# Moving a range check from the second convolution into the output stage of an attention and quantized-convolution kernel

## The chip, the cores and the metric

The kernel runs on one core of a Trainium2 chip, in one launch. The metric is the device time of a run in microseconds (us). Names of engines: PE (TensorE matmul), DVE (VectorE), ACT (ScalarE), POOL (GpSimd), SP (SyncE, which here issues transfers). L1074 means line 1074 of the kernel before; in the kernel after, the lines of the output stage have numbers smaller by three (L1139 is L1136), and those behind it are larger by three (L1326 is L1329).

## The reference

The input x is 16 images of 128 channels and 32 x 32 pixels in float32. Two layers follow each other.

```python
# layer 0: four-head attention over the 1024 pixels of an image
q, k, v = split(einsum('bchw,oc->bohw', x, w_qkv) + b_qkv)
attn = softmax(q @ k * c ** -0.5)
x = einsum(attn @ v, w_out) + b_out + x
# layer 1: two quantized convolutions with batch norm, and a residual
out = conv3x3(act_quant(x), weight_quant(w1))
out = conv3x3(act_quant(batchnorm(out)), weight_quant(w2))
return batchnorm(out) + x
```

The batch norm takes mean and variance over all images, so nothing of the last stage can start before the last image has left the second convolution.

## The kernel before

The softmax is computed without subtracting a maximum, which is exact as long as the sums of exponentials stay in a sane range. The kernel therefore has two paths. `fast_path` computes everything. A check of the reciprocal sums (`check_sums`, L352) writes a flag, and behind `fast_path` every engine loads the flag (L1326) and branches on it (L1327) over `general_attention` and `quantized_convs`, a slower general path that writes the output again. With this input the flag is 0 and all engines take the branch over it.

`fast_path` has four stages. First the attention of 16 images with the first convolution interleaved; it ends at about 1921 us, with the last image's first convolution until 1926. Attention results go to memory (`x_dram`), ten of the first convolution's results too (`y_dram`). Then `bn_params(0)`, and the second convolution from 1929 to 1989.5 us, image by image. Then `bn_params(1)`, and last the output stage: ACT applies scale and bias (L1136, L1138), DVE adds the residual (L1139), SP writes the result (L1140). The residual comes back from memory as `x1` (named `res`), one transfer of 7.5 MB that is under way until about 1957 us.

In the second convolution most images are nine shifted matmuls per half of the image (`conv`, L277, 18 matmuls). Images 3, 5, 7, 9, 11 and 13 are "filtered": four combinations of rows, three matmuls each (`filtered_conv`, L1078). What an image needs is prepared some images ahead by `quantize2(b)` (L1050): ACT writes `steps` (L1058), DVE clips them (L1059), and DVE (L1063, images below 6) or ACT (L1065) writes the padded image, `pad` or, for a filtered one, `padf`. For a filtered image four row combinations follow (L1074), two on DVE and two on POOL. After its matmuls ACT copies an image out of PSUM (L293) or DVE and ACT combine the filtered parts (L1094 to L1098), and DVE takes its statistics (L298).

The order on each engine's queue is not the order of the text alone: a planner places instructions by its estimate of when they can run. `tc.issue_after(x)` holds an instruction behind the instruction x in that order. All queues run in order, so an instruction that waits holds all that stand behind it.

The check consists of eleven small DVE instructions (L349 to L369), one POOL instruction that takes the maximum over the partitions (L371), and one DVE copy of the result into the integer flag (L372). Before POOL's instruction and again before POOL's next row combination the program has an instruction pair that changes POOL's configuration, which the trace shows as MODIFY_POOL_CONFIG under L371 and L1074. The check is called in the loop of the second convolution, behind the statistics of image 1:

```python
if b == 1:
    with tc.issue_after(done.ins):
        check_sums()
```

Of the kernel before, what the change touches and what calls it, by code (L numbers as in the profile page):

```python
# [12 lines left out]
ALU = mybir.AluOpType  # L13
# [180 lines left out]
def fast_path(  # L194
# [18 lines left out]
    B, C, N = x.shape  # L213
# [57 lines left out]
    def gather(n):  # L271
        nc.vector.bn_aggr(late[n][:, 1:3], early[n].rearrange("p g s -> p (g s)"))
        nc.vector.tensor_scalar(
            late[n][:, 2:3], late[n][:, 2:3], float((B - 1) * N), None, ALU.mult
        )

    def conv(pool, tag, b, n, r, rows=RPH, group=None, after=None):  # L277

        ps = pool.tile([P, rows, W], F32, tag=tag, name=f"psc{n}_{b}_{r}")
        for tap in range(NTAP):  # L280
            dy, dx = divmod(tap, 3)
            last = nc.tensor.matmul(  # L282
                ps,
                lhsT=wq[n][:, tap, :],
                rhs=pads[b % NPAD][:, r + dy : r + dy + rows, dx : dx + W],
                start=(tap == 0),
                stop=(tap == NTAP - 1),
            )
        ps = ps.rearrange("p h w -> p (h w)")
        if group is not None:  # L290
            with tc.issue_after(after) if after else nullcontext():
                nc.vector.bn_stats(place(n, b, group), ps)
        nc.scalar.copy(ys[b][:, r * W : (r + rows) * W], ps)  # L293
        return last

    def statistics(b, n):
        for hf in range(NHF):
            last = nc.vector.bn_stats(place(n, b, hf), ys[b][:, ts(hf, HALF)])  # L298
        return last
# [47 lines left out]
    def sums_range(b):  # L347
        flat = sums[:, b * NH : (b + 1) * NH, :].rearrange("p g k -> p (g k)")
        nc.vector.tensor_reduce(ext[:, 0, b : b + 1], flat, AX.X, ALU.min)  # L349
        nc.vector.tensor_reduce(ext[:, 1, b : b + 1], flat, AX.X, ALU.max)  # L350

    def check_sums():  # L352

        sums_range(B - 1)
        ok = keep.tile([P, 2], F32, name="ok")
        low, high = keep.tile([P, 1], F32, name="low"), keep.tile([P, 1], F32, name="high")
        nc.vector.tensor_reduce(low, ext[:, 0, :], AX.X, ALU.min)
        nc.vector.tensor_reduce(high, ext[:, 1, :], AX.X, ALU.max)
        nc.vector.tensor_scalar(ok[:, 0:1], low, 1.0 / SUM_LIMIT, None, ALU.is_ge)
        nc.vector.tensor_scalar(ok[:, 1:2], high, SUM_LIMIT, None, ALU.is_le)  # L360
        bad = keep.tile([P, 1], F32, name="bad")
        nc.vector.tensor_tensor(bad, ok[:, 0:1], ok[:, 1:2], ALU.mult)
        even = keep.tile([P, B], F32, name="even")
        nc.vector.scalar_tensor_tensor(
            even, ext[:, 0, :], SUM_RATIO, ext[:, 1, :], ALU.mult, ALU.is_ge
        )
        nc.vector.tensor_reduce(ok[:, 0:1], even, AX.X, ALU.min)
        nc.vector.tensor_tensor(bad, bad, ok[:, 0:1], ALU.mult)
        nc.vector.tensor_scalar(bad, bad, -1.0, 1.0, ALU.mult, ALU.add)  # L369
        worst = keep.tile([P, 1], F32, name="worst")  # L370
        nc.gpsimd.partition_all_reduce(worst, bad, P, bass_isa.ReduceOp.max)  # L371
        nc.vector.tensor_copy(flag, worst[0:1, :])  # L372

    with ExitStack() as ph:
        pool = lambda name, bufs, **kw: ph.enter_context(tc.tile_pool(name=name, bufs=bufs, **kw))
# [550 lines left out]
        for g in range(LAST):  # L926
            b, h = heads[g]
# [79 lines left out]
    with ExitStack() as ph:  # L1007
# [38 lines left out]
        x1 = resp.tile([P, B, N], F32, name="res")  # L1046
# [3 lines left out]
        def quantize2(b, r0=0, r1=H):  # L1050

            pad = filtered_pads[FILTERED.index(b) % 2] if b in FILTERED else pads[b % NPAD]
            t = steps.tile([P, (r1 - r0) * W], BF16, tag="steps", name="steps")
            y = ys[b][:, r0 * W : r1 * W]
            if (b, r0) == (0, 0):
                nc.vector.tensor_scalar(t, y, scale1, bias1, ALU.mult, ALU.add)
            else:
                nc.scalar.activation(t, y, AF.Identity, bias=bias1, scale=scale1)  # L1058
            nc.vector.tensor_scalar(t, t, STEP, STEP + A_LEVELS, ALU.max, ALU.min)  # L1059
            into = pad[:, r0 + 1 : r1 + 1, 1 : W + 1]  # L1060
            t = t.rearrange("p (h w) -> p h w", w=W)
            if b < 6:
                done = nc.vector.tensor_scalar(into, t, STEP, None, ALU.subtract)  # L1063
            else:
                nc.scalar.activation(into, t, AF.Identity, bias=down)  # L1065
            if b not in FILTERED:
                return done if b < 6 else None
            rows[b] = rowp.tile([P, 4, D, W + 2], BF16, tag="rows", name=f"rows2_{b}")
            pick = lambda r: pad[:, r : r + 2 * D - 1 : 2, :]
            four = ((0, 2, ALU.subtract), (1, 2, ALU.add), (2, 1, ALU.subtract), (1, 3, ALU.subtract))  # L1070
            for k in (1, 2, 0, 3):
                x, y, op = four[k]
                engine = nc.vector if k in (1, 2) else nc.gpsimd
                engine.tensor_tensor(rows[b][:, k], pick(x), pick(y), op)  # L1074
# [3 lines left out]
        def filtered_conv(b):  # L1078
            m = [None] * 4
            for k in (1, 2, 0, 3):  # L1080
                m[k] = ps_c.tile([P, D, W], F32, tag="c", name=f"psf_{b}_{k}")
                for dx in range(3):
                    nc.tensor.matmul(  # L1083
                        m[k],
                        lhsT=weights[k][:, dx, :],
                        rhs=rows[b][:, k, :, dx : dx + W],
                        start=(dx == 0),
                        stop=(dx == 2),
                    )
            y = ys[b].rearrange("p (i r w) -> p r i w", r=2, w=W)  # L1090
            new = lambda what: sump.tile([P, D, W], F32, tag=what, name=f"{what}_{b}")

            half, total = new("half"), new("total")
            nc.scalar.mul(half, m[1], 0.5)  # L1094
            nc.vector.scalar_tensor_tensor(total, m[2], 0.5, half, ALU.mult, ALU.add)
            nc.vector.tensor_tensor(y[:, 0], m[0], total, ALU.add)
            nc.vector.scalar_tensor_tensor(half, m[2], -0.5, half, ALU.mult, ALU.add)
            nc.vector.tensor_tensor(y[:, 1], half, m[3], ALU.subtract)  # L1098
# [8 lines left out]
        for b in range(B):  # L1107
            if b in FILTERED:
                filtered_conv(b)
            else:  # L1110
                ends = starts.get(b, (0, RPH, H))
                for i, (r0, r1) in enumerate(zip(ends, ends[1:])):
                    conv(ps_c, "c", b, 1, r0, r1 - r0, group=i if b == B - 1 else None)
            if b + 2 < B and b + 2 not in FILTERED:
                quantize2(b + 2)
            if b + 4 in FILTERED:
                quantize2(b + 4)
            if b < B - 1:
                done = statistics(b, 1)
            if b == 1:  # L1120
                with tc.issue_after(done.ins):
                    check_sums()
            if b == B - 2:
                gather(1)
        scale2, bias2 = bn_params(1)
# [3 lines left out]
        for b in range(B):  # L1129
            ends = parts.get(b, (0, N))  # L1130
            for lo, hi in zip(ends, ends[1:]):
                y = ys[b][:, lo:hi]
                if b == 0 and hi <= N // 2:
                    nc.vector.tensor_scalar(y, y, scale2, bias2, ALU.mult, ALU.add)
                elif b < 2:
                    nc.scalar.activation(y, y, AF.Identity, bias=bias2, scale=scale2)  # L1136
                elif lo == 0:
                    nc.scalar.activation(ys[b], ys[b], AF.Identity, bias=bias2, scale=scale2)  # L1138
                nc.vector.tensor_tensor(y, y, x1[:, b, lo:hi], ALU.add)  # L1139
                nc.sync.dma_start(out=out[b][:, lo:hi], in_=y)  # L1140
    outer.close()


# [105 lines left out]
def attention_then_quantized_convs(  # L1249
# [49 lines left out]
    def conv_weights(n, wp, behind):  # L1299
# [19 lines left out]

    flag = const.tile([1, 1], mybir.dt.int32, name="flag")  # L1320
    fast_path(
        nc, tc, x, wqk, wvo, bo, bnp, x1d, y1d, out, bo_sb, bnp_sb, quad, wq, sc, flag, conv_weights,
        constants,
# [82 lines left out]
```

## Time and profile before

| what | value |
|---|---|
| median of 3 runs | 2019.51 us (2019.31 to 2022.78) |
| the profiled execution, its own time | 2020.26 us |
| span of the profiled execution | 2018.2 us |
| mean granted TensorE clock | 0.994 |
| busy over the span | PE 98%, DVE 87%, ACT 59%, POOL 1% |
| second convolution, first to last matmul | 1929.2 to 1989.5 us |
| output stage, first output add to last landing | 1992.6 to 2016.8 us |

The span is what the profile sees of one execution; the time of the same execution is 2.06 us longer. Every moment below is counted from the start of the span. "Landing" of a transfer is when its completion is seen; a row of the timeline names at its end, in brackets, how long the engine was idle ahead of it and which instruction ended that. PE's busy share is high over the whole, but the last 90 us have to be read stage by stage.

### The profile page before, as it was taken

To read this page: it belongs to the slowest core of one execution; us is meant where nothing else is said; L and a number is where in the kernel's file an instruction comes from. 1 tells how busy PE (TensorE), PEld (TensorE's weight loads), DVE (VectorE), ACT (ScalarE), POOL (GpSimd) and SP (SyncE) were. 2 spreads that over 40 slices of the span, in tenths; PEclk is the share of its full clock that TensorE was granted. 3 is DMA by queue.
4 is the path that set the end of the run, shared out by engine and by line. 5 is a ranking of instruction groups with operands and counts; after the bars stand their busy time and mean duration, and the time that the engine had idled before them with its cause. 6 is when DMAs were issued, how large, how long until landed. Compare 5 with 4: busy or idle time off the path is not lost.

```text
span 2018.2 us, 25220 instructions
## 1 busy us (share of the span) xinstructions
PE 1980.9 (98%) x9676; PEld 890.9 (44%) x9677; DVE 1746.7 (87%) x2753; ACT 1193.5 (59%) x1992; POOL 19.6 (1%) x29
## 2 busy tenths in 40 slices
PE   9999999999999999999999999999999999999994
PEld 3466444444434444444444444444444444444442
DVE  4889898898988889889888988888898988989888
ACT  3565665665566566566556556656655665665575
POOL 0000000000000000000000000000000000000020
PEclk9999999999999999999999999999999999999997
DMA  1000000000000000000000000000000000000074
GB/s 42 24 1 22 1 22 1 22 1 0 22 0 22 1 7 26 1 21 11 22 11 1 32 1 21 11 21 11 1 32 1 22 11 22 11 1 22 1 281 168
DMA packets 13937, 47.96 MB, mean 24 GB/s; under 512 B 1521, under 2 KB 1905, under 8 KB 13809
## 3 DMA queue, kind: packets, MB, share of 16 engines
q1 hardware_dynamic: 10608, 36.25, 4.8%
q10 hardware_dynamic: 3200, 10.03, 1.6%
q8 instruction: 77, 1.26, 0.3%
q14 instruction: 52, 0.42, 0.1%
HBM read 24.25 MB, written 22.02 MB: 23 GB/s over the span
## 4 chain that ended last, share of the span: by engine, by line
PE 97%; DVE 1%; ACT 0%; issue 0%; DMA 0%; POOL 0%; DVEq 0%; ACTq 0%
PE pss L404 44%; PE psa L404 38%; PE psu L404 6%; PE psv L404 5%; PE psc L282 2%; PE psw L404 2%; PE psf L1083 1%; DVE back L1139 1%; DVE y L1139 0%; DMA x<-in_x_dram 0%; POOL rows L1074 0%; ACT y L1136 0%; PE ps_a L404 0%; PE psr L404 0%; ACT u L510 0%
## 5 line engine op out<-in xcount | busy, mean ns | idle before, releaser
L404 PE MATMUL pss<-u,x 128*64 128x512 f32 (+1 forms) x4128 | 1033.2, 590 | 1.6 <-ACT u L510 1.6
L404 PE MATMUL psa<-e,vo 128*64 128x512 f32 (+1 forms) x3624 | 922.4, 588 | 0.0
L552 ACT ACTIVATE e<-pss 128x512 f32<-128x512 f32 x1008 | 598.0, 597 | 373.4 <-PE pss L404 371.3
L404 PEld LDWEIGHTS pss<-u,x 128*64 128x64 f32 x4128 | 402.1, 137 | 492.3 <-issue 432.7
L404 PEld LDWEIGHTS psa<-e,vo 128*64 128x64 f32 x3624 | 359.9, 137 | 417.8 <-issue 389.5
L556 DVE TENSOR_TENSOR e<-e 128x1024 f32<-128x1024 f32 x252 | 308.1, 1223 | 29.0 <-ACT e L552 21.7
L555 DVE TENSOR_TENSOR e<-e 128x512 f32<-128x512 f32 x252 | 171.5, 680 | 92.2 <-ACT e L552 91.8
L559 DVE TENSOR_TENSOR e<-e 128x512 f32<-128x512 f32 x252 | 173.4, 688 | 18.2 <-DVE e L556 0.5
L596 ACT COPY ev<-psa 128x512 f32<-128x512 f32 x252 | 135.4, 589 | 88.9 <-PE psa L404 87.8
L404 PE MATMUL psu<-x,at_sb 128*64 128x512 f32 x512 | 185.9, 600 | 0.5 <-DMA x<-in_x_dram 0.5
L404 PE MATMUL psv<-bt_sb,x 128*64 128x512 f32 x512 | 184.9, 592 | 1.0 <-ACT bt_sb L481 1.0
L531 ACT COPY vo<-psv 128x512 f32<-128x512 f32 x128 | 75.7, 591 | 142.2 <-PE psv L404 142.2
L565 DVE TENSOR_TENSOR es<-es,e 128x1024 f32<-128x1024 f32 x126 | 154.0, 1222 | 2.2
L510 ACT ACTIVATE u<-psu,au_sb 128x512 f32<-128x512 f32 x127 | 87.6, 690 | 21.2 <-PE psu L404 19.6
L609 DVE TENSOR_TENSOR y<-ev,y 128x512 f32<-128x512 f32 x63 | 43.3, 687 | 52.4 <-ACT y L607 52.4
L404 PEld LDWEIGHTS psv<-bt_sb,x 128*64 128x64 f32 x512 | 58.8, 137 | 63.0 <-issue 55.3
L404 PEld LDWEIGHTS psu<-x,at_sb 128*64 128x64 f32 x512 | 58.9, 138 | 61.5 <-issue 56.8
L665 DVE STREAM_TRANSPOSE rb<-sums 128x1024 f32<-128x1024 f32 (+1 forms) x66 | 80.0, 1211 | 2.1
L835 ACT COPY m<-psw 128x512 f32<-128x512 f32 x45 | 26.4, 587 | 92.4 <-PE psw L404 91.4
L626 DVE TRANSPOSE_TENSOR_REDUCE part<-es 128x32 f32<-128x1024 f32 (+1 forms) x65 | 79.6, 1225 | 0.6
L563 DVE TENSOR_TENSOR es<-e,e 128x1024 f32<-128x1024 f32 x63 | 76.8, 1219 | 0.0
L676 DVE TENSOR_TENSOR av<-av,rb 128x1024 f32<-128x1024 f32 x47 | 57.6, 1225 | 1.6
(165 smaller groups left out, 1234.9 us busy)
## 6 DMA issues: line engine op xcount, KB each, us to landing
x_dram<-acc SPq DMA_DIRECT2D x16, 512.0 KB, 4.2
x<-in_x_dram ACTq DMA_DIRECT2D x15, 512.0 KB, 4.6
res<-x_dram SPq DMA_DIRECT2D x1, 7680.0 KB, 34.4
y_dram<-y SPq DMA_DIRECT2D x10, 512.0 KB, 2.6
back<-y_dram SPq DMA_DIRECT2D x1, 5120.0 KB, 16.6
out_dram<-back SPq DMA_DIRECT2D x10, 512.0 KB, 4.3
out_dram<-y SPq DMA_DIRECT2D x9, 256.0 KB, 2.4
raw<-in_cw_dram ACTq DMA_DIRECT2D x2, 576.0 KB, 4.2
```

Source lines behind the costliest of these rows:

```text
L404: done = nc.tensor.matmul(out_, lhsT=lhsT, rhs=rhs, start=start, stop=stop)
L510: copied = nc.scalar.activation(dst, ps, AF.Identity, bias=au_sb[:, h : h + 1])
L531: nc.scalar.copy(v[:, c : c + 3 : 2], ps.rearrange("p (h a o) -> p a h o", a=2, o=PH))
L552: exps[:] = [nc.scalar.activation(e[:, 2 * c + 1 - m], ps, AF.Exp).ins]
L555: nc.vector.tensor_tensor(e[:, T3], e[:, B12], e[:, B22], ALU.add)
L556: nc.vector.tensor_tensor(e[:, T1 : T2 + 1 : T2 - T1], e[:, B12 : B11 + 1], e[:, B11 : T3 + 1 : T3 - B11], ALU.subtract)
L559: nc.vector.tensor_tensor(e[:, T4], e[:, T2], e[:, B21], ALU.add)
L563: nc.vector.tensor_tensor(sides[g], es[g, 0][:, T4 : T3 + 1], mine, ALU.add)
L565: added = nc.vector.tensor_tensor(sides[g], sides[g], mine, ALU.add)
L596: nc.scalar.copy(to, ps)
L626: nc.vector.tensor_reduce(part, total.rearrange("p (k c) -> p k c", c=Q), AX.X, ALU.add, apply_transpose=True,)
L665: nc.vector.transpose(rb, rinv.unsqueeze(2).to_broadcast([P, n, Q]))
```

## The change

`check_sums` no longer copies the flag; it returns `worst`. Its call moves from the second convolution into the output stage, behind the add of image 4 (B // 4). The copy into the flag follows behind the add of image 13 (B - 3, the fourteenth image). On POOL the all-reduce now stands behind all row combinations, and the configuration is changed once instead of twice. On SP the load of the flag now stands behind all output writes. The new order on DVE in the output stage is: the adds of images 0 to 4; L349, L350, L357; add of image 5; L358, L359, L364, L360; add of 6; L362; add of 7; L367; add of 8; L368; add of 9; L369; adds of 10 to 13; the copy of the flag; adds of 14 and 15. The planner also moves some instructions of the second convolution: DVE's L1059 of image 6 now stands behind L1098 and the second row sum of image 7 and behind the statistics of image 3, where before it stood between L1095 and L1096 of image 3; on ACT L1065 of image 6 stands behind the copies of image 4.

```diff
@@ check_sums
         nc.gpsimd.partition_all_reduce(worst, bad, P, bass_isa.ReduceOp.max)
-        nc.vector.tensor_copy(flag, worst[0:1, :])
+        return worst
@@ the loop of the second convolution
             if b < B - 1:
                 done = statistics(b, 1)
-            if b == 1:
-                with tc.issue_after(done.ins):
-                    check_sums()
             if b == B - 2:
                 gather(1)
@@ the loop of the output stage
-                nc.vector.tensor_tensor(y, y, x1[:, b, lo:hi], ALU.add)
+                added = nc.vector.tensor_tensor(y, y, x1[:, b, lo:hi], ALU.add)
                 nc.sync.dma_start(out=out[b][:, lo:hi], in_=y)
+            if b == B // 4:
+                with tc.issue_after(added.ins):
+                    worst = check_sums()
+            if b == B - 3:
+                with tc.issue_after(added.ins):
+                    nc.vector.tensor_copy(flag, worst[0:1, :])
```

## The prediction

> **What bounds the kernel now.** I read the page first, then the timeline around the check, engine by engine, then the chain, the DMA view and the order of instructions on each queue before and after. The page says the whole is TensorE (PE 98%). The change touches only the last 90 us, so I read PE there. Columns: start us, length us, engine, line, operation, and in brackets the idle time before it and who ended it.
>
> ```profile
> 1941.13 1.48 PE L1083 MATMUL psf<-rows,middle 128*128 128x512 bf16 x6
> 1942.45 1.49 PE L1083 MATMUL psf<-rows,wq 128*128 128x512 bf16 x6
> 1945.52 4.14 PE L282 MATMUL psc<-pad,wq 128*128 128x512 bf16 x18 [1.58 <-DVE pad L1063]
> 1949.50 1.48 PE L1083 MATMUL psf<-rows,middle 128*128 128x512 bf16 x6
> 1952.99 0.82 PE L1083 MATMUL psf<-rows,wq 128*128 128x512 bf16 x3 [2.02 <-POOL rows L1074]
> 1954.27 0.82 PE L1083 MATMUL psf<-rows,wq 128*128 128x512 bf16 x3 [0.45 <-POOL rows L1074]
> 1954.92 4.13 PE L282 MATMUL psc<-pad,wq 128*128 128x512 bf16 x18
> ```
>
> PE waits three times, for image 4's pad and twice for image 5's rows; from 1954.27 to 1989.5 it has no gap. Without waits an 18-matmul image takes 3.97 us in the chain and a filtered one 2.64, so image 4 could have started at 1941.13 + 2.64 = 1943.77 (1.75 lost), image 5's second half at 1945.52 + 3.97 + 1.32 = 1950.81 (2.18 lost), its last three matmuls 0.66 after 1952.99 (0.62 lost): **4.55 us lost**. The DVE and POOL rows say why.
>
> ```profile
> 1940.43 0.43 DVE L1063 TENSOR_SCALAR padf<-steps 128x1024 bf16<-128x1024 bf16 x1
> 1943.15 0.14 DVE L372 CAST flag<-worst 1x1 int32<-1x1 f32 x1 [2.29 <-POOL worst L371]
> 1945.03 0.43 DVE L1063 TENSOR_SCALAR pad<-steps 128x1024 bf16<-128x1024 bf16 x1
> ```
>
> ```profile
> 1932.78 2.42 POOL L1074 TENSOR_TENSOR rows<-padf 128x544 bf16<-128x544 bf16 x2 [1844.81 <-DVE padf L1063]
> 1942.74 0.38 POOL L371 PARTITION_ALL_REDUCE worst<-bad  x1 [7.55 <-issue]
> 1951.82 7.33 POOL L1074 TENSOR_TENSOR rows<-padf 128x544 bf16<-128x544 bf16 x6 [8.71 <-PE psf L1083]
> ```
>
> ```profile
> L371 POOLq MODIFY_POOL_CONFIG  x2: 7/7/7, 1935.4 to 1935.4; - x2
> L1074 POOLq MODIFY_POOL_CONFIG  x4: 83/83/83, 87.9 to 1943.1; - x4
> ```
>
> The flag copy holds DVE for 2.29 us, with image 4's pad four instructions behind. POOL changes its configuration at 1935.4 for the all-reduce and at 1943.1 back for the row sums. Image 5's pad was ready at 1940.86, yet POOL began at 1951.82: the named releaser (PE) is wrong, it is the 8.7 us of the second change. The first took 1935.4 to 1942.74, 7.3 us.
>
> The last stage is set by the output writes. From 1995.00 to 2011.50 the DMA share is 1.01 (395 GB/s) while DVE is also full.
>
> **What the Trainium skill says.** GPSIMD Engine Reference, 2.1 Instruction dispatch: the first call of a freshly loaded kernel pays a load of about 6 us, not visible as an instruction. The trace agrees in kind, with 7.3 and 8.7 us while DMA was full. SBUF — State Buffer, Who interferes with whom: DVE instructions with two SBUF inputs or in a 2-port mode contend with a POOL instruction that reads SBUF. Agrees: DVE's row sums and bf16 L1059 take 0.41 to 0.43 us alone, and when begun under a POOL row sum end 0.29 us after it (1.1 to 1.36 us long). Runtime: NRT & Kernel Launch, Instruction fetch mechanics: a taken branch to a page not held forces a DMA fetch. Agrees, as the next rows show.
>
> ```profile
> L1327 PEldq COMPARE_BRANCH  x1: 3575/3575/3575, 1987.9 to 1987.9; - x1
> L1327 ACTq COMPARE_BRANCH  x1: 54/54/54, 1997.1 to 1997.1; - x1
> L1327 DVEq COMPARE_BRANCH  x1: 72/72/72, 2011.4 to 2011.4; - x1
> L1327 DVEq EVENT_SEMAPHORE  x1: 21/21/21, 2016.2 to 2016.2; - x1
> ```
>
> PE's branch over the rerun takes 3.6 us, with two 16 KB packets of the instruction queue; DVE needs 4.8 us from its branch to its next instruction.
>
> **1. Second convolution, what goes.** Eleven check instructions, the flag copy and its wait, and both configuration changes. I walked DVE, ACT, POOL and PE through the new order with the lengths above (the same walk on the old order puts PE's three late starts at 1945.47, 1953.07 and 1954.27, against 1945.52, 1952.99 and 1954.27). Image 5's L1059 still waits for ACT's steps (1937.85 + 1.24 = 1939.09); its pad lands at 1940.03. POOL starts its rows at 1940.08 instead of 1951.82 and ends at 1942.5; PE needs them at 1949.07, so 6.5 us of cover. DVE's two row sums now collide with POOL and end at 1942.8 (old order: free of POOL, 0.69 us for both); then L1059 and L1063 of image 4 (0.33 and 0.43, and a handover) give its pad at 1943.61. PE wants it at 1943.77: hidden by 0.1 us, thin. **What is late next** is image 6: the new order puts its L1059 behind both row sums of image 7 and image 3's statistics, at 1949.03; ACT's L1065 then runs 1949.5 to 1950.66, PE could start at 1950.38 and starts at 1950.71. That costs 0.3. After it the walk finds no wait, since pads are 3 us early or more. Gain 4.55 − 0.3 = **4.2 us**; bounds 3.6 (image 6 another 0.6 late) and 4.55 (no wait left; PE cannot gain more).
>
> **2. Last stage, what comes on DVE.** In the trace the check's instructions start 0.06 to 0.21 us apart. In the new order three stand before image 5's add (0.49), four before image 6's (0.35), one each before 7 to 10 (0.1 each, their waits on each other covered by the adds between), the copy before image 14's (0.07): 1.3 us; bounds 1.0 and 2.1 (the sum of their lengths). Does this delay the writes? A write lands 1.8 us after issue for 128 KB and 2.1 for 256 KB when the queue is empty, so some 2.8 for 512 KB. Image 5 takes 3.8, images 6 to 10 3.9 to 4.3, the last 5.2: backlogs of 1.0, 1.1 to 1.5, 2.4. DVE's summed delay at those points is 0.49, 0.84 to 1.24, 1.3. So the DMA engines hide it, with 0.1 to 0.5 to spare in the middle; I take **0.2**, bounds 0 and 0.9.
>
> **3. POOL and the flag.** The change to the all-reduce is now queued right after image 13's rows (about 1967) and is done by 1976, with POOL idle; the all-reduce needs it near 2001. From "bad" to the copy lie four adds, 4 × 1.135 = 4.5 us; the all-reduce took 0.4 us here and 1.6 and 0.7 in the weight preparation. Taken: no wait. Behind the copy on DVE stand the adds of images 14 and 15, and SP's last writes wait for those.
>
> **4. The flag's readers.** SP reads the flag (0.47 + 0.18 + 0.03 us) behind its last write instead of at 1943.3; it then waits 4.4 us for landings anyway, so nothing. PE, ACT and POOL read it at about 2006 (image 14's add, 2009.18 − 4.2 + 1.2) and not at 1987.3, 1996.5 and 1969.0. PE's 3.6 to 4.8 us after that end near 2011.5, the last landing is at 2016.77 − 4.2 = 2012.6: hidden by 1 us. But their instruction fetches move into the saturated writes: two 16 KB packets for PE, two of 8 KB for POOL. One DMA engine moves 32 KB of each 512 KB in 1.26 us, so PE's pair holds one engine for up to 1.3 us, and a write lands with its slowest engine. In the old tail the share falls from 1.01 to 0.46 and 0.04 over the last slices, so some engines lag already. Taken **0.5**; bounds 0 (the late ones are others) and 2.0 (all fetches on one engine).
>
> **Sum:** −4.2 + 0.2 + 0.5 = −3.5 us. The profiled execution took 2020.26 us (span 2018.2), 0.75 above the median of 2019.51; off the median that is 2016.0.
>
> **Rivals.** (a) Everything paid later is hidden: −4.1 to −4.55, about 2015.2. For it: DMA backlog and idle PE, ACT, POOL; against it: thin cover in steps 1, 2 and 4. (b) Most is paid back at the end: DVE's delay outruns the backlog (0.9) and the fetches share one engine (2.0): −4.2 + 2.9 = −1.3, 2018.2. The DMA share of 1.01 speaks for it, idle sequencers elsewhere say nothing. (c) Slower: POOL's new configuration is really loaded only at the all-reduce, under saturated writes. Then the copy at DVE waits, images 14 and 15 behind it. If "worst" comes x us after "bad", the cost is x − 4.5 − 1.1 (backlog left) + 0.5; it eats the 4.2 at x = 9.3 and makes the kernel slower beyond. With 8.7 + 0.4 = 9.1 it ends even; with 14 it is 2019.51 + 4.7 = 2024.2. Against it: the first all-reduce of the weights began 0.2 us after its input, 53 us after its configuration (4.9 to 57.8), and L371 started 7.3 us after the configuration, not after "bad".
>
> **How the numbers follow.** Within 0.2% (4.04 us) is about what a measurement of this kernel can tell from no change. My case (−2.5 to −4.04) 0.5, (a) 0.27, (b) 0.15, (c) 0.08, of which 0.04 is over +4.04; 0.02 more for an unseen loss of that size. So faster by over 0.2% 0.27, slower 0.06, same 0.67. The range leaves out the end of (a) beyond −4.7 and nearly all of (c): 2014.8 to 2018.5.
>
> **What would show it.** Right: image 4 on PE at about 1943.8 with no wait, image 6 at 1950.7, the last convolution matmul 4.2 us earlier; POOL's rows of image 5 starting near 1940.1; no idle ahead of the flag copy; the last landing under 5.2 us after its issue. Wrong: an image 6 pad later than 1951.3, DMA share under 0.95 around images 5 to 8, DVE idle at the copy, or a landing of the last image over 5 us with the tail longer than before.

## The result, and the profile after

The kernel after took 2017.31 us (median of 22 runs, 2014.75 to 2019.88), the kernel before on the same chip 2021.03 (22 runs, 2017.72 to 2024.19). The ratio is 0.9983 with a 95% interval of 0.9977 to 0.9989: 3.4 us less (2.2 to 4.6), small but clear of zero. The forecast was 2016.0, with 3.5 us less; it was counted from the median of three runs before (2019.51), which the 22 runs put 1.5 us higher. The profiled execution took 2018.87 us with a span of 2017.1.

Executions of one kernel differ by up to 6.5 us here, and by up to 7.7 in the later runs of the kernel before, in good part ahead of the change: in the profiles of this study the second convolution starts between 1925.9 and 1929.8 us. So the readings below are lengths of stages. **Second convolution** is from its first matmul to the end of the last L292; **tail** is from the end of the L339 behind it (`bias`) to the end of the span. In this profile they are 57.38 and 27.89 us; in the one profile before 60.74 and 26.29. The start is 0.62 us later (1929.83 for 1929.21), which is to be taken off the moments below.

PE after, second convolution, in the same columns as before:

```profile
1941.75 1.48 PE L1083 MATMUL psf<-rows,middle 128*128 128x512 bf16 x6
1943.07 1.49 PE L1083 MATMUL psf<-rows,wq 128*128 128x512 bf16 x6
1944.39 4.13 PE L282 MATMUL psc<-pad,wq 128*128 128x512 bf16 x18
1948.36 1.48 PE L1083 MATMUL psf<-rows,middle 128*128 128x512 bf16 x6
1949.68 1.49 PE L1083 MATMUL psf<-rows,wq 128*128 128x512 bf16 x6
1952.18 4.13 PE L282 MATMUL psc<-pad,wq 128*128 128x512 bf16 x18 [1.02 <-ACT pad L1065]
```

Image 4 (1944.39) and image 5 (1948.36, 1949.68) follow without a wait; only image 6 waits. It starts 2.50 us after 1949.68 where 1.32 would do: 1.18 us lost. POOL after, in the same columns:

```profile
1940.71 2.42 POOL L1074 TENSOR_TENSOR rows<-padf 128x544 bf16<-128x544 bf16 x2 [4.90 <-DVE padf L1063]
2003.13 4.64 POOL L371 PARTITION_ALL_REDUCE worst<-bad  x1 [33.80 <-DVE bad L369]
```

The rows of image 5 come at 1940.71 instead of 1951.82. The all-reduce takes 4.64 us where it took 0.38 before. DVE in the output stage:

```profile
2002.91 4.62 DVE L1136 TENSOR_TENSOR back<-back,res 128x1024 f32<-128x1024 f32 x4
2007.81 0.14 DVE L1143 CAST flag<-worst 1x1 int32<-1x1 f32 x1 [0.28 <-POOL worst L371]
```

DVE reaches the copy at 2007.53 and is idle for only 0.28 us: the four adds last nearly to the end of the all-reduce. The rows of PE's branch and the DMA issues say what the late flag does (minimum, median and maximum in ns, then first and last start; for the issues size and median time to landing; the last row is of the kernel before):

```profile
L1330 PEldq COMPARE_BRANCH  x1: 5072/5072/5072, 2009.3 to 2009.3; - x1
L1330 PEldq EVENT_SEMAPHORE  x1: 51/51/51, 2014.4 to 2014.4; - x1
```

```profile
out_dram<-back SPq DMA_DIRECT2D x10, 512.0 KB, 3.0
out_dram<-y SPq DMA_DIRECT2D x1, 512.0 KB, 5.4
```

```profile
out_dram<-back SPq DMA_DIRECT2D x10, 512.0 KB, 4.3
```

The ten writes in the middle now land after 3.0 us instead of 4.3, so fewer of them queue; yet the last one takes 5.4 us (5.2 before). The step comes late: image 13's write lands after 3.7 us, those of images 14 and 15 after 5.3 and 5.4. The table by windows shows both sides, first of the kernel after, then of the kernel before; the last two columns are the DMA share and GB/s.

```profile
1998.00:2000.00 2.00, 0.00 (x0) 0.00 (x0) 2.00 (x6) 2.00 (x3) 0.00 (x0) 0.50 0.81 326
2000.00:2002.00 2.00, 0.00 (x0) 0.00 (x0) 2.00 (x5) 2.00 (x3) 0.00 (x0) 0.50 0.94 379
...
2013.00:2014.00 1.00, 0.00 (x0) 0.00 (x0) 0.00 (x0) 0.00 (x0) 0.00 (x0) 0.50 0.34 131
2014.00:2015.00 1.00, 0.00 (x0) 0.00 (x0) 0.00 (x0) 0.00 (x0) 0.00 (x0) 0.50 0.09 37
2015.00:2016.00 1.00, 0.00 (x0) 0.00 (x0) 0.00 (x0) 0.00 (x0) 0.00 (x0) 0.50 0.09 16
```

```profile
1998.00:2000.00 2.00, 0.00 (x0) 0.00 (x0) 2.00 (x3) 2.00 (x3) 0.00 (x0) 0.50 0.97 360
2000.00:2002.00 2.00, 0.00 (x0) 0.00 (x0) 2.00 (x3) 2.00 (x2) 0.00 (x0) 0.50 1.04 406
```

At 1998 to 2002 the DMA engines of the kernel after run partly dry: the writes come late from DVE. And from 2014 on a share of 0.09 is left for 1 to 2 us, which is one or two of 16 engines (0.09 × 16 = 1.4) still at work while the others are done.

### The profile page after: what moved, and what is told of

Its sections match the earlier page's. It is cut to its first block, busy times and chain, and to the rows that moved or that the text cites. A ratio compares the mean times of both kernels' runs of the same rounds, so it can differ in the third digit from the quotient of the medians.

```text
span 2017.1 us, 25217 instructions
## 1 busy us (share of the span) xinstructions
PE 1980.9 (98%) x9676; PEld 885.6 (44%) x9677; DVE 1747.5 (87%) x2753; ACT 1191.3 (59%) x1992; POOL 23.6 (1%) x29
## 4 chain that ended last, share of the span: by engine, by line
PE 98%; DVE 1%; ACT 0%; DMA 0%; POOL 0%; ACTq 0%; issue 0%; DVEq 0%
PE pss L404 44%; PE psa L404 38%; PE psu L404 5%; PE psv L404 5%; PE psc L282 2%; PE psw L404 2%; PE psf L1083 1%; DVE back L1136 0%; DMA x<-in_x_dram 0%; DVE y L1136 0%; POOL worst L371 0%; ACT y L1133 0%; PE ps_a L404 0%; PE psr L404 0%; ACT u L510 0%
## 5 line engine op out<-in xcount | busy, mean ns | idle before, releaser
L404 PEld LDWEIGHTS psv<-bt_sb,x 128*64 128x64 f32 x512 | 58.7, 137 | 63.4 <-issue 55.6
```

What stands on the lines that cost most here:

```text
L404: done = nc.tensor.matmul(out_, lhsT=lhsT, rhs=rhs, start=start, stop=stop)
```

## The experiments

The theory to be tested: the gain is POOL's two changes of configuration and the waits behind them; the loss in the tail is DVE's eleven instructions and the late branches with their instruction fetches. The rivals: the gain comes from the eleven instructions leaving a full DVE, or from DVE's wait at the flag alone; the tail's loss is one of the two things and not both. The cuts from the edits leave out lines that only hand on `bad`, `worst` and `summed`; three dots stand for a body that is not shown. Stages of all runs, in us, with the ratio to the kernel before:

| kernel | second convolution | tail | ratio (95% interval) |
|---|---|---|---|
| before, three profiles | 60.74, 61.99, 62.48 | 26.29, 26.25, 26.58 | 1 |
| after | 57.38 | 27.89 | 0.9983 (0.9977 to 0.9989) |
| no_check | 57.40 | 26.61 | 0.9973 (0.9962 to 0.9984) |
| flag_early | 57.38 | 27.10 | 0.9973 (0.9962 to 0.9985) |
| flag_only_late | 57.39 | 27.48 | 0.9981 (0.9971 to 0.9991) |
| check_end_of_conv | 57.94 | 26.53 | 0.9977 (0.9969 to 0.9986) |
| copy_late | 64.18 | 27.44 | 1.0010 (1.0003 to 1.0016) |
| image6_first | 57.86 | 27.91 | 0.9987 (0.9979 to 0.9995) |
| check_mid_image6 | 61.67 | 26.22 | 0.9995 (0.9987 to 1.0003) |
| copy_at_11 | 57.39 | 27.85 | 0.9982 (0.9975 to 0.9990) |
| split | 58.23 | 26.46 | 0.9981 (0.9974 to 0.9987) |
| matmul_max | 58.23 | 26.24 | 0.9979 (0.9973 to 0.9986) |

With early branches and no check in the tail the tail is 26.22 to 26.61 in eight profiles (mean 26.40), so a tenth or two means nothing.

**The tail, taken apart.** no_check is the kernel before without the call of the check, which is the kernel after without the check and its copy:

```diff
-            if b == 1:
-                with tc.issue_after(done.ins):
-                    check_sums()
+    nc.gpsimd.memset(flag, 0)          # ahead of fast_path
```

> Leaves out the whole check; the flag is zero from the start. Two lengths are read in every run: the second convolution (first matmul to the end of the last statistics: 60.74 us before, 57.38 after) and the tail (end of the last batch-norm bias to the end of the span: 26.29 before, 27.89 after). Theory: the convolution gains by losing the flag wait and POOL's configuration changes, and what the tail loses is caused by the check and the flag standing there. So convolution 57.4 (the same order of instructions as after, image 6 still 1.2 late), tail 26.3, time -3.4 us or a ratio of 0.9983. Rival: the tail is longer whatever stands in it, for instance because the writes start in another state: tail 27.5 or more, time about -2.

flag_early is the kernel after with the check's work, but its result goes into a tile nobody reads. The flag stands from the start, so PE and ACT branch early; POOL still branches behind its all-reduce, at 2003.9:

```diff
-                    nc.vector.tensor_copy(flag, worst[0:1, :])
+                    nc.vector.tensor_copy(keep.tile([1, 1], mybir.dt.int32, name="unread_flag"), worst[0:1, :])
+    nc.gpsimd.memset(flag, 0)          # ahead of fast_path
```

> The kernel after, but the flag is zero from the start and the check's result is copied to a tile that nobody reads, so the check's work stays in the output stage and the branches of PE and ACT go back to where they were (POOL's stays behind its all-reduce). It leaves out the use of the check's result. Theory of the fetches: the tail's extra 1.6 us comes mostly from PE's 16 KB instruction fetches among the writes, so the tail is 26.3 to 26.9. Rival, DVE's delay: the last add is 1.4 us later after the bias than before (+21.05 against +19.62) and that is what lengthens the tail, so it stays at 27.6 to 27.9.

flag_only_late is the kernel after with the late copy and without the check:

```diff
+    worst = keep.tile([P, 1], F32, name="worst")
+    nc.gpsimd.memset(worst, 0.0)
-            if b == B // 4: ...
-                    worst = check_sums()
```

> No check at all; the flag is copied from a zeroed tile on DVE behind image 13's add, so all engines branch as late as in the kernel after, and DVE has one small instruction more than with no check. It leaves out the check. Theory of the fetches: tail 27.2 to 27.9, convolution 57.4, time about -2.3. Rival, DVE's delay: tail 26.3 to 26.5, time -3.4.

Measured from no_check (26.61), the check's instructions alone cost 0.5 us (27.10), the late flag alone 0.9 (27.48), both together 1.3 (27.89). Measured from the mean of the eight tails, 26.40, these are 0.7, 1.1 and 1.5: both cost something, and they add up as far as single profiles can tell. The ratios of these runs, whose intervals are 4 us wide, cannot part them. Other runs repeat two of the lengths: 27.44 with the late flag alone (copy_late), 27.85 and 27.91 with both (copy_at_11, image6_first). In flag_early the last add ends 21.05 us after `bias`, as in the kernel after; in no_check and flag_only_late 19.62 and 19.66. So DVE is late by 1.4 us and the DMA engines hide 0.7 to 0.9 of it. The branch in flag_only_late, and that in no_check, where the flag stands from the start:

```profile
L1329 PEldq COMPARE_BRANCH  x1: 5395/5395/5395, 2004.9 to 2004.9; - x1
```

```profile
L1325 PEldq COMPARE_BRANCH  x1: 3675/3675/3675, 1985.1 to 1985.1; - x1
```

Under the saturated writes it takes 1.7 us longer. Most DMA engines are done with the output 23.5 us after `bias` in both, but the last one at 25.54 in flag_only_late and at 24.41 in no_check: the extra microsecond is on one slow engine. The landing times jump from 4.7 us for image 13's write to 6.2 for image 14's in flag_only_late, and go from 4.8 to only 5.1 in no_check. Between these two writes the flag is set, and one of PE's 16 KB instruction packets falls among the writes for 1.1 us. That the slow engine is the one that carried such a packet fits the numbers and is not shown: the trace tells packets by queue and not by engine.

**Which wait of the old order costs the time.** copy_late puts the check back where it was, and leaves only the copy late:

```diff
+            if b == 1:
+                with tc.issue_after(done.ins):
+                    worst = check_sums()
-            if b == B // 4: ...
-                    worst = check_sums()
```

> The check and the all-reduce stand where they stood before (second convolution, behind image 1), only the flag's copy stands behind image 13's add. It tells which of the two waits of the old order cost the time: DVE's 2.3 us at the copy, or POOL's change back to the row sums. If POOL's change is what binds (my theory): image 4 starts without a wait, but image 5's second half still waits for POOL's rows, which come 8 to 9 us after the all-reduce; PE loses about 3 us there, and the second convolution takes 60 to 61 us, as before (60.7); with the late flag's tail of 27.3 to 27.5 us the kernel is up to 1 us slower than before (ratio 1.000 to 1.0005). If DVE's wait binds: the second convolution takes 58.5 us or less and the kernel gains about 1 us.

It is slower than the kernel before. DVE no longer waits for the flag, image 4 starts at 1941.59 without a wait; but PE then runs into POOL's rows sooner and waits longer. POOL and PE of copy_late:

```profile
1940.93 0.48 POOL L371 PARTITION_ALL_REDUCE worst<-bad  x1 [7.94 <-DVE pad L1063]
1951.55 6.96 POOL L1074 TENSOR_TENSOR rows<-padf 128x544 bf16<-128x544 bf16 x6 [10.14 <-issue]
```

```profile
1945.56 1.48 PE L1083 MATMUL psf<-rows,middle 128*128 128x512 bf16 x6
1952.72 2.72 PE L1083 MATMUL psf<-rows,wq 128*128 128x512 bf16 x6 [5.68 <-POOL rows L1074]
1955.23 5.07 PE L282 MATMUL psc<-pad,wq 128*128 128x512 bf16 x18
```

So the change back to the row sums binds; to take away the flag's wait alone gains nothing. The stage is 3.4 us longer than in the first profile before, where the theory expected about the same: the change took 10.1 us here and not 8.7, and after the long wait six matmuls take 2.72 us instead of 1.49. The windows of copy_late (the column ahead of the DMA share is the granted TensorE clock) show the clock at half. It fell at 1950.34, within the wait, and rose at 1957.17, so PE's first 4.4 us of work behind the wait ran at half:

```profile
1952.00:1954.00 2.00, 1.28 (x4) 0.44 (x4) 0.00 (x0) 0.20 (x1) 2.00 (x3) 0.50 1.01 406
1954.00:1956.00 2.00, 2.00 (x6) 0.70 (x5) 1.74 (x3) 2.00 (x3) 2.00 (x3) 0.50 0.81 320
1956.00:1958.00 2.00, 2.00 (x8) 0.79 (x7) 2.00 (x4) 1.12 (x1) 2.00 (x2) 0.71 0.01 4
1958.00:1960.00 2.00, 2.00 (x11) 0.89 (x10) 1.74 (x4) 1.64 (x2) 0.51 (x1) 1.00 0.00 0
```

**POOL's configuration or DVE's instructions.** matmul_max is the kernel before with POOL's all-reduce exchanged for a matmul with a column of ones (`one`); with it the write of the flag moves from behind image 1 to behind image 2:

```diff
-        nc.gpsimd.partition_all_reduce(worst, bad, P, bass_isa.ReduceOp.max)
-        nc.vector.tensor_copy(flag, worst[0:1, :])
+            if b == 2:
+                many = ps_c.tile([1, 1], F32, tag="c", name="many")
+                nc.tensor.matmul(many, lhsT=bad, rhs=one, start=True, stop=True)
+                with tc.issue_after(done.ins):
+                    nc.vector.tensor_scalar(flag, many, 1.0, None, ALU.min)
```

> The kernel before with one thing exchanged: the maximum over partitions is a matmul of 'bad' with a column of ones (sum over partitions, limited to 1) instead of POOL's all-reduce, so POOL never changes its configuration; check and flag copy stay in the second convolution, behind images 1 and 2. If POOL's configuration is the cause of the old order's waits: no wait for image 5's rows, second convolution 57.5 to 58.5 us, tail 26.3 to 26.6, 2.5 to 3.3 us less than before. If DVE's check instructions or the early flag is the cause: it stays above 59.5 us.

split keeps the all-reduce, but behind POOL's last row sums, so that there is one change of configuration and not two:

```diff
+            if b == 1:
+                with tc.issue_after(done.ins):
+                    bad = check_sums()
+            if b == 9:
+                with tc.issue_after(summed[3].ins):      # POOL's last row sum of image 13
+                    nc.gpsimd.partition_all_reduce(worst, bad, P, bass_isa.ReduceOp.max)
+            if b == 14:
+                with tc.issue_after(done.ins):
+                    nc.vector.tensor_copy(flag, worst[0:1, :])
```

> The check's DVE instructions stand where the kernel before has them (second convolution, behind image 1's statistics), but the all-reduce comes behind POOL's last row sums, so that POOL changes its configuration once, and the copy of the flag behind image 14's statistics. If the old order's loss was POOL's change and DVE's wait for it (what the runs so far point to), and not the eleven instructions: DVE has 0.95 us idle right there in the kernel after (0.51 and 0.44 at 1938.6 and 1939.7), the eleven need about 1.5, so the second convolution takes 57.4 to 58.3 us (before 60.7) and the tail 26.3 to 26.6, ratio 0.9975 to 0.9983. If the instructions themselves cost the old order its time: 59.5 us or more in the second convolution and a ratio near 0.999.

Both give 58.23 us. PE of matmul_max:

```profile
1941.30 4.14 PE L282 MATMUL psc<-pad,wq 128*128 128x512 bf16 x18 [0.42 <-DVE pad L1063]
1945.28 1.48 PE L1083 MATMUL psf<-rows,middle 128*128 128x512 bf16 x6
1946.60 1.49 PE L1083 MATMUL psf<-rows,wq 128*128 128x512 bf16 x6
1949.12 4.13 PE L282 MATMUL psc<-pad,wq 128*128 128x512 bf16 x18 [1.04 <-ACT pad L1065]
```

The wait for image 5's rows is gone, while check and flag stay early. The 0.85 us above the kernel after's 57.38 are what the eleven instructions cost at their old place (image 4 starts 0.6 to 0.8 us late); what the kernel before takes above 58.23 goes with POOL's configuration and the waits for it.

**How long the old stage really is.** The stages of the first profile before explain only 1.8 us of the 3.4 (3.36 less in the convolution, 1.60 more in the tail). So the kernel before was profiled twice more, one execution each (2018.94 and 2019.24 us).

> The kernel before once more, one profiled execution. The stage lengths of the profiled pair explain 1.8 us (second convolution 60.74 to 57.38, tail 26.29 to 27.89), the medians differ by 3.4 to 3.7. Theory: the length of POOL's change of configuration varies from execution to execution (8.7 us in the profile before, 10.1 in the run with only the copy late), so that the second convolution of the kernel before is often longer than in its one profile: 61.5 us or more here. Rival: the stage is as before, 60.7 within 0.2, and the rest lies ahead of it (start of the second convolution 1 us or more later than in the other kernels' profiles, 1925.9 to 1929.8) or outside the span.

> As for the run ahead of it, a second profiled execution of the kernel before: 61.5 us or more in the second convolution if POOL's change of configuration varies and is often longer than in the first profile; 60.7 within 0.2 if it does not.

```profile
1943.62 5.79 PE L282 MATMUL psc<-pad,wq 128*128 128x512 bf16 x18 [2.08 <-DVE pad L1063]
1951.84 0.82 PE L1083 MATMUL psf<-rows,wq 128*128 128x512 bf16 x3 [1.11 <-POOL rows L1074]
```

```profile
1939.06 0.38 POOL L371 PARTITION_ALL_REDUCE worst<-bad  x1 [6.90 <-issue]
1948.82 7.20 POOL L1074 TENSOR_TENSOR rows<-padf 128x544 bf16<-128x544 bf16 x6 [9.38 <-issue]
```

The first fence is PE of before_2, the second POOL of before_3. In before_2 image 4 waits 2.24 us and its 18 matmuls then take 5.79 instead of 4.13, at half clock; in before_3 the change back takes 9.4 us, PE waits 3.1 and is slow afterwards. The stage is 61.99 and 62.48, against 60.74 in the profile that the forecast was made from; in the nine profiles of other kernels in which POOL's rows are in time and DVE keeps up it stays between 57.38 and 58.23. The mean of the three is 61.74, so the stage gained some 4.4 us, and 4.4 less 1.5 in the tail (27.89 against a mean of 26.37) is 2.8. Another 0.2 to 0.3 lies outside the span: time less span is 2.1 us before and 1.8 after in the medians. That makes 3.0 to 3.1 of 3.4 us, inside the interval, if the stages ahead of the change last equally long on average, which these few profiles can't show. The other kernels speak for the mean of the three: taken from it, the sums of their two stages put ten of the eleven ratios in the table inside their intervals (copy_late is outside by 0.0001); taken from the first profile alone, two.

**Image 6, and what binds behind it.** image6_first calls the preparation of image 6 ahead of that of image 7:

```diff
+            if b == 3:
+                quantize2(6)
-            if b + 2 < B and b + 2 not in FILTERED:
+            if b + 2 < B and b + 2 not in FILTERED and b != 4:
```

> The kernel after, with image 6's preparation called ahead of image 7's. My theory of image 6's wait: its L1059 stood on DVE behind image 7's row sums and image 3's statistics. Then PE's 1.19 us ahead of image 6 go to 0 to 0.2, and the second convolution takes 56.2 to 56.6 us instead of 57.4; the tail stays at 27.9. Rival: ACT or DVE has no room at all there and the wait moves to image 7 or to image 4's combination; then it stays at 57.2 us or more.

The first half of the theory came true, PE's wait is gone:

```profile
1949.30 1.49 PE L1083 MATMUL psf<-rows,wq 128*128 128x512 bf16 x6
1950.62 4.13 PE L282 MATMUL psc<-pad,wq 128*128 128x512 bf16 x18
```

But the stage is 57.86 and not 56.4. Its end on DVE, first in the kernel after, then in image6_first:

```profile
1985.21 1.02 DVE L292 BATCH_NORM_STATS2 late<-psc 128x6 f32<-128x512 f32 x2
1986.78 0.43 DVE L292 BATCH_NORM_STATS2 late<-psc 128x6 f32<-128x256 f32 x1 [0.56 <-PE psc L282]
```

```profile
1985.78 1.35 DVE L292 BATCH_NORM_STATS2 late<-psc 128x6 f32<-128x512 f32 x3
```

In the kernel after DVE waits 0.56 us for the last matmul; with image 6 first PE is done early and DVE is late, with no idle time ahead of its last L292. What used up this slack on DVE is a collision that the new order makes. POOL begins its row sums of an image at 1967.48, and a clip begun just behind takes 1.29 us and not 0.4:

```profile
1967.60 1.29 DVE L1059 TENSOR_SCALAR steps<-steps 128x1024 bf16<-128x1024 bf16 x1
```

DVE's own row sums add 0.3 us, so its busy time in the stage grows from 54.6 to 55.6 us, and it had 0.56 to give. The rival's number was right, its place was not: the time is lost at the stage's end. check_end_of_conv shows the same bound with the check behind image 11's statistics (and the copy behind image 14's):

```diff
+            if b == 11:
+                with tc.issue_after(done.ins):
+                    worst = check_sums()
+            if b == 14:
+                with tc.issue_after(done.ins):
+                    nc.vector.tensor_copy(flag, worst[0:1, :])
```

> The check stands in the second convolution behind image 11's statistics, its all-reduce behind all of POOL's row sums, the flag's copy behind image 14's statistics, so nothing of it is in the output stage. Theory: convolution 57.4 to 57.8 (DVE has slack behind image 11; the all-reduce is loaded by then), tail 26.3, time -3.1 to -3.4. Rival: DVE is too full there, or the all-reduce takes 4.6 us here as well and holds the copy: convolution 58.5 or more, time -2.2 or less.

It took 57.94 us, 0.56 more, with a tail of 26.53. check_mid_image6 was to join what seemed good, image 6 first and the check behind image 6's statistics:

```diff
+            if b == 3:
+                quantize2(6)
+            if b == 6:
+                with tc.issue_after(done.ins):
+                    bad = check_sums()
+            if b == 9:
+                with tc.issue_after(summed[3].ins):
+                    nc.gpsimd.partition_all_reduce(worst, bad, P, bass_isa.ReduceOp.max)
+            if b == 13: ...                  # copy of the flag
```

> What the runs so far point to: image 6 prepared ahead of image 7; the check's DVE instructions in the second convolution behind the statistics of image 6; the all-reduce behind POOL's rows of image 13, so that POOL changes its configuration once; the copy of the flag behind the statistics of image 13. Expected if the costs add up as the single runs showed: second convolution 56.2 to 56.8 us, tail 26.3 to 26.6 (no check work in the output stage, early branches), together 4.3 to 4.6 us less than before, ratio 0.9977 to 0.9979. Rival: DVE has no slack in the middle of the second convolution either, the check's instructions delay pads, and the second convolution takes 57.5 us or more.

It missed by 5 us. PE of check_mid_image6 (the lines of that kernel are two smaller):

```profile
1959.53 1.49 PE L1081 MATMUL psf<-rows,wq 128*128 128x512 bf16 x6
1964.65 5.79 PE L282 MATMUL psc<-pad,wq 128*128 128x512 bf16 x18 [3.64 <-ACT pad L1063]
```

Here DVE works without a pause from 1944 to 1968 with the check among the preparations of images 9 and 10; the clip of image 10 comes at 1963.01, 2.2 us after PE wanted the image. Image 10 starts 3.8 us late, and half clock follows again (5.79 for 18 matmuls), which costs another 1.7. The rival was right: there is no slack in the middle.

**Why the all-reduce took 4.64 us.** copy_at_11 is the kernel after with the flag's copy two adds earlier:

```diff
-            if b == B - 3:
+            if b == B - 5:
```

> The kernel after, with the flag's copy two adds earlier, behind image 11's. It asks why the all-reduce took 4.64 us in the output stage and 0.38 in the second convolution. If DVE's back-to-back adds hold POOL out (port theory), the all-reduce ends about 0.25 us after DVE comes to stand at the copy, lasts some 2.3 to 2.5 us, and DVE's idle time at the copy stays near 0.3 us. If the all-reduce needs its 4.6 us by itself there (its program or its load under saturated writes), it lasts 4.6 us again and DVE stands at the copy for about 2.5 us, which then delays the last two writes and lengthens the tail of 27.9 us by up to 1.5.

POOL and DVE of copy_at_11:

```profile
2000.15 2.37 POOL L371 PARTITION_ALL_REDUCE worst<-bad  x1 [33.79 <-DVE bad L369]
```

```profile
1999.93 2.35 DVE L1136 TENSOR_TENSOR back<-back,res 128x1024 f32<-128x1024 f32 x2
2002.56 0.14 DVE L1143 CAST flag<-worst 1x1 int32<-1x1 f32 x1 [0.28 <-POOL worst L371]
```

With two adds ahead of the copy instead of four it lasts 2.37 us. In both kernels it ends 0.25 us after DVE stops (2002.52 against 2002.28; 2007.78 against 2007.53). It needs no 4.6 us; it waits for DVE to stop adding. Nothing is gained by the earlier copy (0.9982 for 0.9983). The jump in the landing times moves with the copy: here it lies between the writes of images 11 and 12 (3.4 and 5.1 us) and no longer between 13 and 14. So it belongs to what the flag sets off.

Of the kernels that keep the check and its decision, check_end_of_conv, matmul_max and split have the smallest sums of both stages (84.5 to 84.7 us, against 85.3 after), but their intervals overlap with that of the kernel after; none was shown to be better.

## Why the prediction was right, and where it was not

The number was right, in part by luck. Two errors in the second convolution cancelled (0.9 us one way, 1.0 the other), and the tail cost 1.5 us where 0.7 was forecast; against that stand 0.2 to 0.3 us outside the span and about 0.3 that neither explains. All four signs that were set down for being wrong came true: image 6's pad at 1951.5 with the later start taken off (1951.3 was the limit), a DMA share of 0.81, DVE idle at the copy for 0.28 us, and a last landing over 5 us with a longer tail.

- **Step 1, direction and places: right.** POOL's rows of image 5 at 1940.71 (forecast 1940.1, and the start is 0.62 later), image 4 at 1944.39 without a wait (1943.8), image 6 late next.
- **Step 1, size of image 6's wait: wrong**, 1.18 us for 0.3. The failed step is the moment of its L1059: 1949.03, or 1949.65 with the later start, and it came at 1950.54. DVE after:

```profile
1947.13 1.34 DVE L1074 TENSOR_TENSOR rows<-padf 128x544 bf16<-128x544 bf16 x1
1948.40 0.68 DVE L1098 TENSOR_TENSOR y<-half,psf 128x512 f32<-128x512 f32 x1
1949.00 0.43 DVE L1074 TENSOR_TENSOR rows<-padf 128x544 bf16<-128x544 bf16 x1
1949.35 1.27 DVE L298 BATCH_NORM_STATS2 early<-y 128x6 f32<-128x512 f32 x2
1950.54 0.40 DVE L1059 TENSOR_SCALAR steps<-steps 128x1024 bf16<-128x1024 bf16 x1
```

  The first row sum of image 7 takes 1.34 us and not 0.43, since POOL has begun its own of that image at 1945.96 and holds it up until 1948.18. The prediction had stated this collision and applied it to image 5's rows, but not to image 7's. These 0.91 us are the miss: 4.55 lost before, less 1.18, is 3.37, and the two profiles differ by 3.36, which is under the lower bound of 3.6.
- **Step 1, the 4.55 us themselves** were read from one execution in which POOL's change took 8.7 us and PE's clock stayed up. Three profiles average 1.0 us more. That error has the opposite sign to the one on image 6.
- **Step 2: the delay right, its cover too thick.** DVE is 1.43 us later at its last add (forecast 1.3), but the end moves by 0.5 to 0.7, not 0.2. The backlogs at images 6 to 10, read from landing times, were taken as full cover; the DMA share of 0.81 at 1998 to 2000, around image 5's add, shows that it was used up there.
- **Step 3: right in effect.** DVE idles 0.28 us at the copy, so rival (c) is out. The all-reduce's 0.4 us was wrong by a factor of twelve, and the cover of four adds on which the step rested was not the reason: the all-reduce ends 0.25 us after DVE stops, behind two adds as behind four.
- **Step 4: the branches hidden, the fetches underrated.** PE comes out of its branch at 2014.4, 1.2 us ahead of the last landing, as forecast. The late flag costs 0.9 to 1.1 us instead of 0.5, within the bounds. The sign set down for it, a last landing over 5 us, says little alone: it was 5.2 before and 5.5 in no_check. The jump between two images says more.
- **The rivals.** (a) is out: the tail pays 1.3 to 1.5 us. Half of (b)'s 2.9 us of repayment is real: +1.5. Against the one profile of before alone it would have looked the likeliest (1.8 us of gain); the lost time before, about 1.2 and 1.7 us larger in the other two profiles, makes the difference.

On the Trainium skill: GPSIMD Engine Reference, 2.1 Instruction dispatch, puts the load that the first call of a freshly loaded kernel pays at about 6 us. Here POOL's idle times lie at 6.9 to 8.0 us ahead of the all-reduce and at 8.7 to 10.1 ahead of the row sums behind it, in four profiles with a DMA share of about 1. In split the change to the all-reduce comes with the DMA share at 0.00, and the idle time is close to the page's figure (5.9 in check_mid_image6):

```profile
1972.87 0.38 POOL L1124 PARTITION_ALL_REDUCE worst<-bad  x1 [6.20 <-issue]
```

So the change cost about 6 us where no transfers ran, and more beside full DMA; that the transfers are the reason was not tested alone. The forecast took the one pair of 7.3 and 8.7, and one profile can't show that it spreads.

## What to carry to other kernels

A single small POOL instruction of another kind, put among regular POOL work, costs a change of configuration there and back, and here the second change was the one that bound; put it behind the last regular POOL instruction, or do the maximum with a matmul. When a wait goes, count the next two waits with the collisions that the new order makes, and ask how much idle time the engine behind them has left (here 0.56 us). Work moved into a stage bound by output writes is not free: late data and the late flag with its instruction fetches both reached the end here.

## What the runs showed of the hardware that was not expected

- **Half clock after a wait.** Where PE started 2.2, 3.1 and 3.8 us late (before_2, before_3, check_mid_image6) the granted clock fell to 0.5 for 3.4 us, from 0.2 to 1.7 us after the start on, which costs 1.6 to 1.7 us on 18 matmuls; where it started 5.8 us late (copy_late) the 6.8 us at half began within the wait. After waits of 1.2, 1.75 and 2.18 us it did not. The Trainium skill (TensorE: Matmul & The Clock Gate, Part 1) tells of half clock after an idle window of about 3.4 us that runs free of the program; the length agrees, but 2.1 us of idle time were enough in before_2. So a wait of about 2 us or more can cost nearly twice its length, in some executions and not in others.
- **An all-reduce that waits for DVE.** Beside back-to-back adds with two SBUF inputs the POOL all-reduce lasts as long as the adds do, plus 0.25 us (0.38 to 4.64 us). The Trainium skill (SBUF — State Buffer, Who interferes with whom) names such adds as contending with a POOL instruction that reads SBUF, and calls the ports they share an exclusive lock; in these runs the moments between two adds did not let the all-reduce end either.
- **The change of configuration varies** with nothing in the program: 8.71, 9.45 and 9.38 us in three executions of the kernel before at the same place, 10.14 in copy_late.
